# A two-layer convolution kernel: one image's rows on another engine, stores on another queue, two loads swapped, statistics spread over more steps, one sum placed later

## The chip, the cores and the metric

The kernel runs on one core of a Trainium2 chip. The core has five engines with an instruction queue each: TensorE (PE, with its weight loads listed as PEld), VectorE (DVE), ScalarE (ACT), GpSimd (POOL) and SyncE (SP). SP does nothing but issue transfers[...]. All transfers are carried by the same 16 DMA engines. Each engine works through its own queue in order, and waits on semaphores for what others produce.

The metric is the device time of one execution in microseconds (us). The time before is the median of three runs, 2894.33 us (2892.17 to 2900.01).

## The reference

The input `x` has 4 images of 16 channels with 256 by 256 points. Two layers follow each other, each with a group normalization (8 groups of 2 channels) in front and its input added behind:

```python
def _L0_conv_ref(x, conv_w, conv_b):          # conv_w: 400 x 16 x 3 x 3
    out = conv(x, conv_w, padding='SAME') + conv_b[None, :, None, None]
    logits = out.reshape(N, C, K * K, H, W)   # C = 16, K = 5
    weights = jax.nn.softmax(logits, axis=2)
    return jnp.einsum('ncuij,ncuij->ncij', _unfold(x), weights)
...
def _L1_conv_ref(x, base_weight, spline_weight, spline_scaler, bias_weight):
    patches = _extract_patches(x, 3, 1, 1)
    bspl = _b_splines(patches, grid)          # 8 cubic B-splines on a grid of step 0.4
    out = jnp.einsum('bjhwn,ijn->bihw', jax.nn.silu(patches), base_weight.sum(axis=2))
    out = out + jnp.einsum('bjhwns,ijns->bihw', bspl,
                           (spline_weight * spline_scaler[..., None]).sum(axis=2))
    return out + bias_weight[None, :, None, None]
...
x = x + _L0_conv_ref(_gn(x), L0_conv_conv_w, L0_conv_conv_b)
x = x + _L1_conv_ref(_gn(x), L1_conv_base_weight, ...)
```

In layer 0, every point of every channel has 25 logits from a 3x3 convolution; their softmax weights the 5x5 neighbourhood of the normalized point. In what follows, h is the normalized x.

## The kernel before

**Stages.** A set-up loads x and the weights, takes the statistics of images 0 and 1, and normalizes the upper half of image 0. Layer 0 then runs over 64 strips: 4 images, 2 halves of 128 rows, 8 strips of 32 columns. Layer 1 runs over units of 16 rows. A second copy of both layers, for logits too large for a plain exponential, stands behind a branch that these inputs don't take.

**What normalization leaves.** h goes to DRAM scratch in two layouts, by `normalize` (L383). Rows, `hs`: tiles `hsp` are computed by ScalarE at L460 (two channels of a row for all strips with their margins, 128x576), the outer margins are copied from `zpad` (L469, L470), and `put_rows` (L416) stores them. Columns, `hst` and `hsl`: `ht` (L473) is transposed on TensorE into `tp` (L498), copied to `tt` and, rounded, to `hi` (L489), their difference is `lo`, and `put_columns` (L430) stores the three. Edges of the scratch are filled with zeros by the transfers of `zeros` (L399), 13 an image.

**Set-up.** SP issues the loads of x and of the weights, GpSimd those of layer 1's weights (`sw`, `ss`, `bw`, 31 transfers). VectorE takes bn_stats of image 0, then `group_stats` and `factors` give the scale and bias `nrm` (L243 to L246). Then the code calls `zeros(0)` on GpSimd's queue, `prepare0` (layer 0's weights, which GpSimd rearranges at L653 and L654), starts normalizing image 0, takes image 1's bn_stats with steps of that normalization in between, and calls `prepare1` (layer 1's weights: GpSimd's product at L619 and L666, 12 stores `ws<-wb` at L689). How the instructions of the set-up stand on an engine beyond the data they need is left to the framework's scheduler.

**A strip of layer 0.** Eight steps of four columns, 512 steps in all. In a step TensorE computes the logits of the four columns in two halves (L1023 on `am`, the taps of `hst`, L1027 on `an`, the taps of `hsl`, with a row of ones for the bias in `an`, filled at L773), into three PSUM buffers. ScalarE takes the exponential of each half (L1046) into one of four buffers `e`. GpSimd multiplies it with `u`, the rows of h (L1051). VectorE sums e and e times u over the 25 taps (L850) one step behind (`LAG = 1`). At a strip's end a quotient follows: ScalarE sums the denominators with a `Copy` (L864), takes `Ln` (L867) and `Exp` (L869), VectorE does L875, L879 and L886. Every four strips `y` is added to a block `xc` of x and stored to `x1s` in two transfers (L958), and ScalarE takes its statistics for layer 1 with pairs of `z` (L921).

`load_im` loads `am` and `an` for 16 columns (four transfers L787, one L795; for the very first in two halves) and `load_u` loads u for a strip (L808), all in SP's queue, ahead of their use.

**Beside the strips** a generator `ahead` issues one piece of other work a step: the lower half of image 0, then image 1's normalization, and for images 2 and 3 first `measure` (L248), then normalization. `measure` lets ScalarE form sums and squares of x by rows of a partition; at its end TensorE sums them over partitions (product with `ones`), VectorE forms the mean and the deviations `dev` (L290 to L298), TensorE sums these (L300), VectorE forms the variance (L304, L307), GpSimd raises it to the power −1/2 (L309), and `factors` makes `nrm` and `nrz`. A `yield` between them moves what follows by one step, in the queues of all engines.

**Order.** From layer 0 on, `in_order` binds each engine to the order of the program text. `behind(i, name)` puts one instruction behind another. `seeds[0]`, `seeds[1]` and `seeds[2]` name ScalarE's, GpSimd's and VectorE's first instruction of the last strip's end that is put behind the start of layer 1: `seeds[0]`, at L868, is the `Ln` of L867.

Of the kernel before, what the change touches and what calls it, by code (L numbers as in the profile page):

```python
# [34 lines left out]
def conv_preact_kernel(  # L35
# [212 lines left out]
    def measure(b, ptr, tiles, busy):  # L248
        xps = tiles[1]
        n = GC * W  # L250

        def load(q, h):
            if q < C // QC:
                nc.sync.dma_start(
                    xps[h][:, :, PAD : PAD + W],
                    x[b, q * QC : (q + 1) * QC, h * P : (h + 1) * P, :].rearrange(
                        "c p w -> p c w"),
                )

        for h in range(NH):  # L260
            load(0, h)
        for _ in range(3):
            yield
        for q in range(C // QC):
            for h in range(NH):
                for k in range(QC // GC):
                    while busy():
                        yield
                    g = q * (QC // GC) + k
                    v = xps[h][:, k * GC : (k + 1) * GC, PAD : PAD + W]  # L270
                    m, s = (moments[:, t, g, h : h + 1] for t in range(2))
                    nc.scalar.activation(v, v, AF.Identity, accum_out=s)
                    nc.scalar.activation(m, s, AF.Copy, scale=-1.0 / n)
                    nc.scalar.activation(v, v, AF.Square, bias=m, accum_out=s)
                    yield
                load(q + 1, h)

        def small(k, name):
            return stat1.tile([P, k], F32, name=f"{name}_{b}", tag=f"{name}m")

        d = stat1.tile([P, G, NH], F32, name=f"dev_{b}", tag="dev")
        mean, var, rstd = small(G, "mean"), small(G, "var"), small(G, "rstd")
        bank = ptr.tile([P, QG, P], F32, name=f"mps_{b}", tag="tp")
        ps = [bank[:, k, 0 : G * NH] for k in range(2)]
        nc.tensor.matmul(
            ps[0], lhsT=ones, rhs=moments[:, 0].rearrange("p g h -> p (g h)"),
            start=True, stop=True,
        )
        yield
        nc.vector.tensor_reduce(  # L290
            mean, ps[0].rearrange("p (g h) -> p g h", h=NH), AX.X, ALU.add
        )
        nc.vector.tensor_scalar(mean, mean, -1.0 / NH, None, ALU.mult)
        nc.vector.tensor_tensor(
            d, moments[:, 0], mean.unsqueeze(2).to_broadcast([P, G, NH]), ALU.add
        )
        nc.vector.tensor_mul(d, d, d)
        nc.vector.scalar_tensor_tensor(d, moments[:, 1], 1.0 / n, d, ALU.mult, ALU.add)  # L298
        yield
        nc.tensor.matmul(  # L300
            ps[1], lhsT=ones, rhs=d.rearrange("p g h -> p (g h)"), start=True, stop=True
        )
        yield
        nc.vector.tensor_reduce(  # L304
            var, ps[1].rearrange("p (g h) -> p g h", h=NH), AX.X, ALU.add
        )
        nc.vector.tensor_scalar(var, var, 1.0 / NH, EPS, ALU.mult, ALU.add)  # L307
        yield
        nc.gpsimd.tensor_tensor(rstd, var, mhalf, ALU.pow)  # L309
        yield  # L310
        factors(b, mean, rstd)
        yield
# [70 lines left out]
    def normalize(b, ptr, tiles, held=None, copier=None, part=None, dense=False):  # L383
# [64 lines left out]
        def rows(q):  # L448
            for h in read:
                xp = place(q, h) if held is None else held[h][:, q * QC : (q + 1) * QC]  # L450
                if part != 1:
                    hsp = prep.tile([P, NST, QC, SP], F32, name=f"hsp{b}_{q}_{h}", tag="hsp")
                ht = prep.tile([P, QW, W // QW, QC], F32, name=f"ht{b}_{q}_{h}", tag=f"ht{h}")
                hts[q, h] = ht
                for k in range(QC // GC):
                    g = q * (QC // GC) + k
                    kc = slice(k * GC, (k + 1) * GC)
                    how = dict(scale=nrm[b][:, 0, g : g + 1], bias=nrm[b][:, 1, g : g + 1])
                    if part != 1:
                        nc.scalar.activation(  # L460
                            hsp[:, :, kc, :].rearrange("p s c w -> p c s w"),
                            bass.AP(
                                tensor=xp.tensor, offset=xp.offset + k * GC * (W + 2 * PAD),
                                ap=[xp.ap[0], [W + 2 * PAD, GC], [SW, NST], [1, SP]],
                            ),
                            AF.Identity, **how,
                        )
                        if k == QC // GC - 1:
                            nc.scalar.copy(hsp[:, 0, :, 0:PAD], zpad)  # L469
                            nc.scalar.copy(hsp[:, NST - 1, :, PAD + SW :], zpad)  # L470
                            moves.append((4, partial(put_rows, q, h, hsp)))
                        yield
                    nc.scalar.activation(  # L473
                        ht[:, :, :, kc].rearrange("p g w c -> p c w g"),
                        xp[:, kc, PAD : PAD + W].rearrange("p c (w g) -> p c w g", g=QW),
                        AF.Identity, **how,
                    )
                    if k == QC // GC - 1:
                        moves.append((4, partial(load, q + (1 if part is None else 2), h)))
                    yield  # L480
# [85 lines left out]
    with tc.tile_pool(name="prep0", bufs=2) as prep, tc.tile_pool(  # L566
# [43 lines left out]
            )  # L610
        for r in range(2):
            nc.sync.dma_start(wnr[r : r + 1, :], conv_b)
        nm = 3 * C
        sw = pre.tile([P, 3, 9, nm], F32, name="sw")
        ss = pre.tile([P, 3, 9, nm], F32, name="ss")
# [48 lines left out]
        def prepare1():  # L664

            nc.gpsimd.tensor_mul(sw, sw, ss)  # L666
            wc = pre.tile([P, 3, nm], F32, name="wc")
            for d in range(3):
                nc.vector.tensor_reduce(
                    wc[:, d], sw[:, d].rearrange("p k j -> p j k"), AX.X, ALU.add  # L670
                )
            nc.vector.tensor_scalar(wc, wc, -1.0 / 6.0, None, ALU.mult)
            order = pre.tile([P, 2, C, SH], F32, name="order")
            nc.vector.tensor_copy(order, ident.rearrange("p (c h s) -> p h c s", h=2, s=SH))
            wcp = ptr0.tile([P, QG, P], F32, name="wcp", tag="tp").rearrange("p g w -> p (g w)")
            wcp = wcp[:, 0 : 3 * nm]
            nc.tensor.matmul(
                wcp, lhsT=order.rearrange("p h c s -> p (h c s)"),
                rhs=wc.rearrange("p d j -> p (d j)"), start=True, stop=True,
            )  # L680
            wb1 = pre.tile([nm, nm], F32, name="wb1")
            nc.vector.tensor_reduce(wb1, bw.rearrange("p k j -> p j k"), AX.X, ALU.add)
            for r in range(RT):
                nc.vector.tensor_copy(
                    wt[:, r : r + 3, :, r, :], wcp.rearrange("p (d e o) -> p d e o", d=3, e=3)
                )
                for d in range(3):
                    for h in range(2):
                        nc.sync.dma_start(  # L689
                            ws[h * (P // 2) + r + d : (h + 1) * (P // 2) : RD, h, :, r, :],  # L690
                            wb1[d * C : (d + 1) * C].rearrange("p (e o) -> p e o", e=3),
                        )
# [5 lines left out]
        for b in range(2):  # L698
# [16 lines left out]
            mean, rstd = group_stats(stat, pstat, st, f"x{b}")  # L715
            factors(b, mean, rstd)
            if b == 0:
                for f in zeros(0, nc.gpsimd):
                    f()
                prepare0()  # L720
            if b == 1:
                prepare1()
            if b == 0:
                ahead = normalize(0, ptr0, tiles, held, nc.vector.tensor_copy, 0)
# [33 lines left out]
    def layer0(shift):  # L758
# [4 lines left out]
        with tc.tile_pool(name=f"prep{arm}", bufs=2) as prep, tc.tile_pool(  # L763
# [6 lines left out]
            ans = [imp.tile([KT, CI * RP], F32R, name=f"an{n}{arm}", bufs=1) for n in range(NIM)]  # L770
            for t in ans:

                nc.vector.memset(t.bitcast(F32)[0 : 2 * C], 1.0)  # L773
            tiles = norm_tiles(prep)
            strips = [(b, hf, s) for b in range(B) for hf in range(NH) for s in range(NST)]
            nci = SW // CI
# [85 lines left out]
            def seed(n, nd, xc):  # L862
                r = prc.tile([P, C, SW], F32, name=f"r_{n}{arm}", tag="r")
                nc.scalar.activation(  # L864
                    nd[:, 0], nd[:, 0], AF.Copy, accum_out=seen[:, 1, n : n + 1]
                )
                nc.scalar.activation(r, nd[:, 0], AF.Ln, bias=tiny)  # L867
                seeds[:1] = [newest(ACTE)]  # L868
                nc.scalar.activation(  # L869
                    r, r, AF.Exp, scale=-1.0, accum_out=seen[:, 0, n : n + 1]  # L870
                )
                after(1, divide, n, nd, xc, r)
# [78 lines left out]
            def store(n, xc):  # L951
# [16 lines left out]
                    ),  # L968
                )
            )  # L970
            ims = [load_im(0)]
            us = [load_u(0)]
            y = None
            ahead = iter(())
            for n, (b, hf, s) in enumerate(strips):
# [511 lines left out]
```

## Time and profile before

The profiled execution took 2882.99 us; the program's span in it is 2881.0, with 1.99 around it. The median of the three runs is 11.3 us above it.

| what | from | value |
|---|---|---|
| set-up, to the first sum of layer 0 | start of the first L850 | 102.6 us |
| layer 0 | 102.6 to 2002.5 us | 1899.9 us |
| layer 1 | 2002.5 us to the end | 878.5 us |
| busy: PE, DVE, ACT, POOL | page, part 1 | 2691.3, 2763.2, 2204.9, 2665.2 us |
| TensorE's granted clock in the set-up, layer 0, layer 1 | busy times by stage | 0.83, 0.99, 0.98 |
| first am load, first product of TensorE, first exponential | time line | 82.97, 87.68, 91.68 us |
| u of the first strip: issued; first product e times u | time line | 89.52; 99.05 us |

A line of the page's groups reads: line, engine, operation, output <- input, shape, count | busy time, mean of one in ns | idle time of the engine just before, and what ended it. A line of the time line reads: start and length in us, engine, line, operation, names, count, and in brackets the idle time before it with what ended it. A line of the list of waits reads: engine, its instruction <- what it waited for: us in total, times, longest us. "SPq" is SP issuing a transfer, "PEld" a weight load. The table of stages has, for each stretch, its length and the busy time of PE, PEld, DVE, ACT and POOL, then the granted clock, the share of the DMA engines and GB/s.

### The profile page before, as it was taken

What the parts mean: (1) busy time and instruction counts of PE and PEld (TensorE: products, weight loads), DVE (VectorE), ACT (ScalarE), POOL (GpSimd) and SP (SyncE); (2) the same over time, 40 slices, a digit from 0 to 9 for tenths busy, and PEclk for the clock granted to TensorE, in tenths of its full rate; (3) what the DMA queues carried; (4) which work ended last, traced back from release to release, by engine and by line L of the source; (5) the groups of instructions that cost most, each with busy time, mean ns of one, the idle gap of its engine ahead of it and who ended that gap; (6) DMA issues with size and microseconds to landing.
All of it is one profiled execution on the core that took longest, in us unless ns stands there. A gap on an engine that the chain in (4) does not pass through costs nothing.

```text
span 2881.0 us, 39240 instructions
## 1 busy us (share of the span) xinstructions
PE 2691.3 (93%) x14150; PEld 1486.9 (52%) x14150; DVE 2763.2 (96%) x1735; ACT 2204.9 (77%) x3077; POOL 2665.2 (93%) x1096
## 2 busy tenths in 40 slices
PE   2798999998999999899999999995899999999998
PEld 1465666655665666566666666663243343343232
DVE  5699999999999999999999999998999999999996
ACT  5466887686877678688664655647999999999995
POOL 4698999998998999899999999999899999999995
PEclk9899999999999999999999999998999999999999
DMA  8878999985999878699986674865787887787883
GB/s 248 253 244 231 280 288 273 273 245 174 276 289 298 247 231 244 197 307 278 283 252 189 196 225 152 242 195 176 234 250 252 247 251 251 239 261 247 252 250 99
DMA packets 337856, 692.96 MB, mean 241 GB/s; under 512 B 29746, under 2 KB 254468, under 8 KB 287284
## 3 DMA queue, kind: packets, MB, share of 16 engines
q1 hardware_dynamic: 329988, 658.13, 73.8%
q0 software_dynamic: 7664, 32.23, 5.5%
q8 instruction: 114, 1.87, 0.3%
q14 instruction: 90, 0.74, 0.1%
HBM read 533.16 MB, written 121.15 MB: 227 GB/s over the span
## 4 chain that ended last, share of the span: by engine, by line
DVE 47%; PE 23%; issue 10%; ACT 7%; DMA 7%; POOL 5%; SPq 1%; DVEq 0%; ACTq 0%; POOLq 0%
DVE nd L850 36%; PE yp L1353 10%; PE lg L1023 8%; POOL e L1051 3%; DVE ring L182 3%; DVE s L179 3%; PE yp L1362 2%; PE lg L1027 2%; ACT xtc L1188 1%; DVE r1a L1197 1%; ACT xtb L1188 1%; DMA an<-hsl 1%; DVE nd L875 1%; DVE r L879 1%; DVE y L886 1%
## 5 line engine op out<-in xcount | busy, mean ns | idle before, releaser
L1051 POOL TENSOR_TENSOR e<-e,u 128x1600 f32<-128x1600 f32 x512 | 1804.6, 3799 | 77.8 <-ACT e L1046 63.3
L850 DVE TENSOR_REDUCE nd<-e 128x128 f32<-128x3200 f32 x512 | 1757.1, 3476 | 46.8 <-POOL e L1051 46.5
L1023 PE MATMUL lg<-wm,am 128*128 128x400 f32 x4096 | 1738.1, 505 | 65.4 <-ACT e L1046 42.3
L1027 PE MATMUL lg<-wn,an 96*128 96x400 f32 x2048 | 1346.8, 658 | 3.5 <-DMA an<-hsl 3.4
L1046 ACT ACTIVATE e<-lg 128x800 f32<-128x800 f32 x1024 | 823.6, 835 | 548.0 <-DVE nd L850 277.9
L1023 PEld LDWEIGHTS lg<-wm,am 128*128 128x128 f32 x4096 | 760.8, 192 | 388.7 <-ACT e L1046 89.4
L1353 PE MATMUL yp<-ring,wt 128*32 128x512 f32 x6144 | 715.9, 594 | 39.9 <-DVE ring L182 37.5
L1027 PEld LDWEIGHTS lg<-wn,an 96*128 96x128 f32 x2048 | 388.1, 190 | 317.2 <-DMA an<-hsl 12.1
L1353 PEld LDWEIGHTS yp<-ring,wt 128*32 128x32 f32 x6144 | 239.3, 108 | 483.9 <-issue 414.0
L1210 POOL TENSOR_TENSOR s1b<-s1b,r1a 128x1024 f32<-128x1024 f32 (+1 forms) x96 | 192.4, 2039 | 0.0
L1210 POOL TENSOR_TENSOR s1a<-s1a,r1a 128x1024 f32<-128x1024 f32 (+1 forms) x96 | 192.2, 2035 | 0.0
L182 DVE SCALAR_TENSOR_TENSOR ring<-s,s1a 128x1024 f32<-128x1024 f32 x132 | 154.7, 1191 | 0.9
L182 DVE SCALAR_TENSOR_TENSOR ring<-s,s1b 128x1024 f32<-128x1024 f32 (+1 forms) x128 | 151.7, 1206 | 0.3
L921 ACT ACTIVATE z<-xc,nrm 128x256 f32<-128x256 f32 x240 | 143.7, 599 | 4.0
L1210 POOL TENSOR_TENSOR s1a<-s1a,r1b 128x512 f32<-128x512 f32 (+2 forms) x68 | 119.7, 1789 | 2.8 <-ACT s1a L1203 2.8
L1210 POOL TENSOR_TENSOR s1b<-s1b,r1b 128x512 f32<-128x512 f32 x64 | 114.9, 1822 | 0.0
L179 DVE SCALAR_TENSOR_TENSOR s<-xta,cb,s 128x1024 f32<-128x1024 f32 (+2 forms) x90 | 111.1, 1255 | 0.5 <-DMA slb<-x1s 0.4
L1206 POOL TENSOR_TENSOR s1a<-r1b 128x1536 f32<-128x1536 f32 (+1 forms) x31 | 86.6, 2794 | 24.5 <-ACT r1b L1195 24.5
L1206 POOL TENSOR_TENSOR s1b<-r1b 128x1536 f32<-128x1536 f32 (+1 forms) x32 | 86.4, 2700 | 22.5 <-ACT r1b L1195 22.5
L179 DVE SCALAR_TENSOR_TENSOR s<-xtb,cb,s 128x1024 f32<-128x1024 f32 (+2 forms) x85 | 105.9, 1266 | 0.2 <-ACT s L176 0.2
L176 ACT ACTIVATE s<-xta,cb 128x1024 f32<-128x1024 f32 (+2 forms) x90 | 96.5, 1086 | 12.5 <-DVE ring L182 11.0
L179 DVE SCALAR_TENSOR_TENSOR s<-xtc,cb,s 128x1024 f32<-128x1024 f32 (+2 forms) x85 | 105.8, 1266 | 0.0
(209 smaller groups left out, 2275.3 us busy)
## 6 DMA issues: line engine op xcount, KB each, us to landing
am<-hst SPq DMA_DIRECT2D x508, 259.8 KB
u<-hs SPq DMA_DIRECT2D x64, 1440.0 KB
an<-hsl SPq DMA_DIRECT2D x127, 519.5 KB
xta<-x1s SPq DMA_DIRECT2D x40, 1024.0 KB
xtb<-x1s SPq DMA_DIRECT2D x40, 1024.0 KB
xtc<-x1s SPq DMA_DIRECT2D x40, 1024.0 KB
x1s<-xc SPq DMA_DIRECT2D x30, 1024.0 KB
xp<-in_x_dram SPq DMA_DIRECT2D x44, 512.0 KB
```

The costliest lines, as they stand in the source:

```text
L176: nc.scalar.activation(s, t, AF.Square, scale=-0.5, bias=cb)
L179: nc.vector.scalar_tensor_tensor(p, t, cb2, s, ALU.subtract, ALU.mult)
L182: nc.vector.scalar_tensor_tensor(f, p, 0.0, q, ALU.min, op)
L850: nc.vector.tensor_reduce(nd[:, :, :, j : j + JG].rearrange("p t c j -> p t j c"), e.rearrange("p t j m c d -> p t j c m d"), AX.XY, ALU.add,)
L921: nc.scalar.activation(z, v, f, scale=nrm[b][:, 0, g : g + 1], bias=nrm[b][:, 1, g : g + 1], accum_out=st1[b][:, t, g, columns_of(n) : col ...
L1023: nc.tensor.matmul(lg[:, i, :NL], lhsT=am[:, o : o + P], rhs=wm.rearrange("p m c d -> p (m c d)"), start=True, stop=False,)
L1027: nc.tensor.matmul(lg[:, i, :NL], lhsT=an[:, o : o + P], rhs=wn.rearrange("p m c d -> p (m c d)"), start=False, stop=True,)
L1046: nc.scalar.activation(ev, lg[:, :, :NL], AF.Exp)
L1051: nc.gpsimd.tensor_tensor(e[:, 1].rearrange("p j m c d -> p j (m c) d"), e[:, 0].rearrange("p j m c d -> p j (m c) d"), uv, ALU.mult,)
L1206: nc.gpsimd.tensor_tensor(s1(n, a, z), r1(n, a, z), r1(n, a, z), ALU.mult)
L1210: nc.gpsimd.tensor_tensor(s1(n, a, z), s1(n, a, z), r1(n, a, z), ALU.mult)
L1353: nc.tensor.matmul(yp[t * M : (t + 1) * M], lhsT=wt[:, d, e].rearrange("p r o -> p (r o)"), rhs=ring[:, r0 + t * RT + d : r0 + t * RT + d ...
```

## The change

It has five parts, and the line numbers after it are up to 14 higher.

1. Image 0's rows `hsp` of the set-up (`part == 0`) are computed by GpSimd, with `tensor_scalar` in place of ScalarE's `activation`, and their margins are set by GpSimd's `memset`. `zeros(0)` is called earlier, ahead of the loads of `sw`, `ss` and `bw` in GpSimd's queue. `prepare0` is called after the factors of image 1 in place of image 0. The fill of `an` with ones moves from VectorE to GpSimd.
2. The 12 stores of `ws` go from SP's queue to GpSimd's.
3. `load_u(0)` is called before `load_im(0)`.
4. In `measure`, the four groups of the end stand 2, 4, 2 and 4 steps apart; before, 1 step each. What follows, image 2's and image 3's normalization, comes eight steps later.
5. `seeds[0]` is the `Copy` with the sum of the denominators, no longer the `Ln`: the last strip's sum stands behind ScalarE's start of layer 1 too.

```diff
@@ measure
         yield
+        yield
         nc.vector.tensor_reduce(
             mean, ps[0].rearrange("p (g h) -> p g h", h=NH), AX.X, ALU.add
         )
...
         nc.vector.scalar_tensor_tensor(d, moments[:, 1], 1.0 / n, d, ALU.mult, ALU.add)
-        yield
+        for _ in range(4):
+            yield
         nc.tensor.matmul(
             ps[1], lhsT=ones, rhs=d.rearrange("p g h -> p (g h)"), start=True, stop=True
         )
+        yield
         yield
         nc.vector.tensor_reduce(
             var, ps[1].rearrange("p (g h) -> p g h", h=NH), AX.X, ALU.add
         )
         nc.vector.tensor_scalar(var, var, 1.0 / NH, EPS, ALU.mult, ALU.add)
-        yield
+        for _ in range(4):
+            yield
         nc.gpsimd.tensor_tensor(rstd, var, mhalf, ALU.pow)
@@ normalize, rows
                     if part != 1:
-                        nc.scalar.activation(
-                            hsp[:, :, kc, :].rearrange("p s c w -> p c s w"),
-                            bass.AP(
...
-                            ),
-                            AF.Identity, **how,
+                        to = hsp[:, :, kc, :].rearrange("p s c w -> p c s w")
+                        row = bass.AP(
...
                         )
+                        if part == 0:
+                            nc.gpsimd.tensor_scalar(
+                                to, row, how["scale"], how["bias"], ALU.mult, ALU.add
+                            )
+                        else:
+                            nc.scalar.activation(to, row, AF.Identity, **how)
                         if k == QC // GC - 1:
-                            nc.scalar.copy(hsp[:, 0, :, 0:PAD], zpad)
-                            nc.scalar.copy(hsp[:, NST - 1, :, PAD + SW :], zpad)
+                            for v in (hsp[:, 0, :, 0:PAD], hsp[:, NST - 1, :, PAD + SW :]):
+                                if part == 0:
+                                    nc.gpsimd.memset(v, 0.0)
+                                else:
+                                    nc.scalar.copy(v, zpad)
@@ set-up
             nc.sync.dma_start(wnr[r : r + 1, :], conv_b)
+        for z in zeros(0, nc.gpsimd):
+            z()
         nm = 3 * C
...
-                        nc.sync.dma_start(
+                        nc.gpsimd.dma_start(
                             ws[h * (P // 2) + r + d : (h + 1) * (P // 2) : RD, h, :, r, :],
...
             if b == 0:
-                for f in zeros(0, nc.gpsimd):
-                    f()
+                pass
+            if b == 1:
                 prepare0()
-            if b == 1:
                 prepare1()
@@ layer0
-                nc.vector.memset(t.bitcast(F32)[0 : 2 * C], 1.0)
+                nc.gpsimd.memset(t.bitcast(F32)[0 : 2 * C], 1.0)
...
                     nd[:, 0], nd[:, 0], AF.Copy, accum_out=seen[:, 1, n : n + 1]
                 )
+                seeds[:1] = [[
+                    i for i in nc.cur_bb.bb.instructions[-8:] if i.engine == ACTE
+                    and isinstance(i, mybir.InstActivation)
+                ][-1]]
                 nc.scalar.activation(r, nd[:, 0], AF.Ln, bias=tiny)
-                seeds[:1] = [newest(ACTE)]
...
+            us = [load_u(0)]
             ims = [load_im(0)]
-            us = [load_u(0)]
```

## The prediction

> **What bounds the kernel.** I read the busy shares of the page first, then the chain that ended last, then busy times by stage, and then the time lines of the places that the change touches. Of the page:
>
> ```profile
> DVE 47%; PE 23%; issue 10%; ACT 7%; DMA 7%; POOL 5%; SPq 1%; DVEq 0%; ACTq 0%; POOLq 0%
> ...
> L1051 POOL TENSOR_TENSOR e<-e,u 128x1600 f32<-128x1600 f32 x512 | 1804.6, 3799 | 77.8 <-ACT e L1046 63.3
> L850 DVE TENSOR_REDUCE nd<-e 128x128 f32<-128x3200 f32 x512 | 1757.1, 3476 | 46.8 <-POOL e L1051 46.5
> ```
>
> In the table by stages, set-up ends at 102.6 us, with the first reduction, and layer 0 fills what follows up to 2002.5:
>
> ```profile
> 102.60:2002.50 1899.90, 1812.12 (x6344) 1167.42 (x6342) 1875.85 (x753) 1332.94 (x2393) 1832.82 (x569) 0.99 0.81 242
> ```
>
> The third pair is VectorE: 1875.85 of 1899.90 us. GpSimd, the fifth, has 1832.82. VectorE bounds layer 0; GpSimd is 2% behind. A quiet strip takes 28.94 us, eight reductions (3.39 from start to start) and three operations of 0.59. What lengthens VectorE's queue there lengthens the run; what empties another engine's queue costs only as far as VectorE runs dry.
>
> The statistics of image 2, on VectorE:
>
> ```profile
> 678.09 3.48 DVE L850 TENSOR_REDUCE nd<-e 128x128 f32<-128x3200 f32 x1
> 681.48 0.17 DVE L290 TENSOR_REDUCE mean<-mps 128x8 f32<-128x16 f32 x1
> 681.69 0.17 DVE L293 TENSOR_SCALAR mean<-mean 128x8 f32<-128x8 f32 x1
> ...
> 682.31 0.17 DVE L298 SCALAR_TENSOR_TENSOR dev<-moments,dev 128x16 f32<-128x16 f32 x1
> 682.40 3.48 DVE L850 TENSOR_REDUCE nd<-e 128x128 f32<-128x3200 f32 x1
> ...
> 690.58 2.78 DVE L307 TENSOR_SCALAR var<-var 128x8 f32<-128x8 f32 x1
> 693.38 3.49 DVE L850 TENSOR_REDUCE nd<-e 128x128 f32<-128x3200 f32 x1
> ...
> 700.77 1.22 DVE L243 COPY nrm<-rstd 128x8 f32<-128x8 f32 x1
> 701.91 0.24 DVE L244 SCALAR_TENSOR_TENSOR nrm<-mean,rstd 128x8 f32<-128x8 f32 x1
> 702.07 3.56 DVE L246 SCALAR_TENSOR_TENSOR nrz<-rstd 128x8 f32<-128x8 f32 x1
> 705.56 3.48 DVE L850 TENSOR_REDUCE nd<-e 128x128 f32<-128x3200 f32 x1
> ```
>
> and on GpSimd at that time:
>
> ```profile
> 689.82 7.01 POOL L1051 TENSOR_TENSOR e<-e,u 128x1600 f32<-128x1600 f32 x2 [8.98 <-ACT e L1046]
> ...
> 698.43 3.53 POOL L1051 TENSOR_TENSOR e<-e,u 128x1600 f32<-128x1600 f32 x1
> ...
> 702.09 6.99 POOL L1051 TENSOR_TENSOR e<-e,u 128x1600 f32<-128x1600 f32 x2
> ```
>
> The reader is to see two things. VectorE never stands idle: its loss in this strip is 0.92 (681.48 to 682.40), 3.00 (690.38 to 693.38) and 4.79 (700.77 to 705.56), 8.71 in all, which is the strip's length, 37.65, less 28.94. And operations on eight elements take 0.17 us while GpSimd stands idle but 1.22, 2.78 and 3.56 while it works, each ending where a GpSimd product ends (693.33, 701.96, 705.6). The same holds for image 3.
>
> **What the Trainium skill says.** "SBUF — State Buffer", section "SBUF: two separate sides": VectorE and GpSimd share one pair of ports as an exclusive lock; a VectorE operation in a two-port mode, or with two SBUF inputs, waits for the whole GpSimd instruction that holds it. The lines above agree (L246: 3.56; in set-up, with GpSimd idle, 0.15). L1197 doesn't: it too reads two SBUF tensors, one a broadcast column, beside a GpSimd busy nine tenths of the time, and its longest is 1.28 against 1.27 in the median. So not every form is held. "VectorE: DVE Perf Modes", section "The perf-mode tier table", puts float32 copies and tensor_scalar from SBUF in a two-port mode, and a PSUM operand outside it; L243 and L307 were held, L290 and L304 (PSUM) took 0.17.
>
> **The change, part by part.** From the list of waits:
>
> ```profile
> PE mps L300 <- DVE dev L298: 14.7, 2, 7.8
> POOL e L1051 <- DMA u<-hs: 13.9, 1, 13.9
> DVE nd L875 <- ACT r L869: 7.6, 1, 7.6
> ```
>
> *Statistics further apart.* TensorE's product of the deviations is issued one step after the mean, while TensorE runs some three steps ahead of VectorE, so it waited 7.8 and 6.9 us, and GpSimd starved for 8.98 and 7.47. With four steps between them this wait goes. But the starvation cost VectorE only what it waited for a product, about 2.6 us, and it spent that in L307, held until 693.36. In exchange, L293 to L298 ran free because GpSimd was starved; now they meet a busy one. New sum for an image. First group: own time 0.92; L293, of L307's form, half a product (3.5/2 = 1.75); L297 and L298 have two SBUF inputs like L246, and GpSimd takes its next product as soon as one ends, so each can wait a whole one: 3.3 or 6.6. L294 reads a broadcast as L1197 does, so nothing. 6.0 to 9.3. Second group (L304, L307): 0.4 + 1.75 = 2.1. Third (L243, L244, L246): 1.75 + 0.24 + 3.5 = 5.5, L246 as before since GpSimd's L245 still stands just ahead of it. 13.6 to 16.9, less 8.7: +5 to +8. While VectorE is held no e comes free (four buffers), so a third hold finds GpSimd out of work now and then: I take +7, for two images +14. Bounds: +1.5 an image if neither L297 nor L298 is held, and another 2 less if the phases are kind; +8.5 at most. So −1 to +17.
>
> *Normalization of images 2 and 3, eight steps later.* Strips 27 and 43 lost 6.6 and 4.7 us where SP's queue backed up: at 877 to 911 stores of x1s, a put of rows behind ACT's z, zeros (8.17 us in issue) and puts of columns stood ahead of am and an. In the new order the columns meet these bursts twice, in strips 27 and 31, as they did before in 23 (no loss) and 27. I cost it at nothing; bounds −12 (the loss gone) and +10 (another of some 5 us at each image's end, where the last puts now stand just ahead of the next image's loads).
>
> *Rows of image 0 on GpSimd, weight stores on its queue, zeros first, prepare0 later, an's fill.* This takes 16 × 0.855 us (L460) and 16 small copies off ACT, from SP the issues below, and from VectorE two fills of 1.79.
>
> ```profile
> 51.90 8.47 SPq L689 DMA_DIRECT2D ws<-wb  x12
> ```
>
> Against that, VectorE's order now puts image 1's bn_stats ahead of image 0's nrm, so normalization begins only behind image 1's second load (landed at 36.4) and its bn_stats, near 41 us, and not at 33.6; and all rows run in GpSimd's queue behind the weights' preparation. A tensor_scalar of 128x576 isn't in the trace. GpSimd's copies of 258 and 34 elements took 0.39 and 0.24, 0.69 ns an element, so 0.6 for 576; its two-input products take 2.1 ns an element, 1.4. "GPSIMD Engine Reference", section 3.1, has one-input bodies at 1.03 to 1.8 cycles of 1.2 GHz: an estimate of 0.6 to 1.0 with dispatch. I take 0.8. Following the queues with the trace's durations, the last put of columns, which landed at 82.8, lands at 81 (79.8 for 0.6; 83.3 for 1.1; 86.9 for 1.4): −1.8, bounds −3 and +4. GpSimd's queue: zeros' 13 issues now stand before the weights, the 12 stores of some 0.5 behind them; only layer 1 needs these stores.
>
> *u ahead of am.* u was issued at 89.52 after eight am loads and landed 9.4 later; GpSimd waited 13.9 in all. The second exponential of the first product ended at 95.2, so at most 99.05 − 95.3 = 3.8 is to be had; then ACT is what is late. Two am transfers now share the engines with u: I take −3.2, bounds −3.8 and 0. Set-up together: −5, bounds −7 and +4.
>
> *The last strip's sum.* ACT stood 5.5 us on it, and VectorE 7.57 at L875. But layer 1's first VectorE operation reads:
>
> ```profile
> 2012.84 1.29 DVE L179 SCALAR_TENSOR_TENSOR s<-xta,cb,s 128x1024 f32<-128x1024 f32 x1 [0.42 <-DMA slb<-x1s]
> ```
>
> slb's loads are issued once the last reduction ends (2002.53), which doesn't move, and land at 2012.85. So VectorE's 7.6 us become a wait for slb: −0.5, bounds −3 and 0.
>
> Sum: −5 + 14 + 0 − 0.5 = +8.5. Against the profiled execution, 2882.99 (span 2881.0, 1.99 around it), that is 2891.5; the median of the runs, 2894.33, is 11.3 higher, so 2903.
>
> **The rivals.**
> - *A, the forecast*, +8.5, 2903; its own range −1 to +17.
> - *B, the forms of the first group are hardly held*: 2 × 1.5 in place of 14, −5 − 0.5: −2.5, 2892. For it: L1197. Against: L246.
> - *C, the other side: SP's queue.* If rows and columns fall clear of the bursts, the stalls of strips 27 and 43 go (−12), with a lock cost in the middle (+6) and set-up −6: −12, 2882. It decides as soon as the gain there passes the lock's cost less 6. For it: in 23 the same burst cost nothing. Against: the put of rows still stands in the burst of strip 27.
> - *D, the last puts meet the burst of strip 31* ahead of the next image's first loads: +5 an image on top of A: +18, 2912. For it: SP's long issues at 894 to 902. Against: no zeros, rows or x are left in that burst.
> - That the yields don't move the product far enough: excluded by the new order, where it stands four steps behind the deviations.
>
> **How the numbers follow.** Chances: A 0.50, B 0.10, C 0.24, D 0.16. 0.3% is 8.7 us, about what a measurement of this kernel can tell from no change. Three fifths of A's chance lies beyond it, the rest within: slower 0.30 + 0.16 = 0.46; same 0.20 + 0.10 = 0.30; faster 0.24. Range 2880 to 2917: it leaves out the lower part of C and the upper of D.
>
> **What would show it.** Right: no wait of TensorE on dev, GpSimd busy through strip 19, and L293, L297, L298, L307, L243, L246 at 1 to 3.6 us, strips 19 to 21 together 13 to 17 us above three quiet ones. Wrong: L297 and L298 at 0.17 beside a working GpSimd; strips 27 and 43 at 29; a GpSimd row over 1.1 us, or the first product later than 96; L179 at the start of layer 1 ahead of slb.

## The result, and the profile after

The changed kernel took 2902.27 us in the median of 17 runs (2895.95 to 2910.16), the kernel before 2891.99 in 17 runs beside them. The ratio is 1.0036, 95% interval 1.0022 to 1.0050: some 10 us slower, 6 to 14 by the interval. The profiled execution has a span of 2901.5 us against 2881.0. That pair lies 20.5 us apart, more than the medians do, so its parts are read for where time goes, and their sum is not the result. Where a part also varies between executions of kernels that have it alike, the other profiles are named beside it.

From the first sum of layer 0 on, both kernels are compared strip by strip (the time between the starts of the strips' first reductions; a quiet strip takes 28.94 us). The excess of a strip over that, in the two profiles:

| part | before | changed | difference |
|---|---|---|---|
| set-up, to the first sum of layer 0 | 102.6 | 101.3 | −1.3 |
| strips 19 and 20 (statistics of image 2) | 8.7 | 11.2 | +2.5 |
| strips 35 and 36 (statistics of image 3) | 8.0 | 13.8 | +5.8 |
| strips 27 and 43 | 11.3 | 15.2 | +3.9 |
| strips 31, 34 and 47 | 0.0 | 9.0 | +9.0 |
| last sum of layer 0 to layer 1's first L179 (start to start) | 13.8 | 8.5 | −5.3 |
| the rest of layer 1 | 868.2 | 874.7 | +6.5 |

First the places that the prediction showed. VectorE's time line in the changed kernel, the statistics of image 2 (L291 to L310 are L290 to L307 of the kernel before), and below it GpSimd's:

```profile
683.19 0.17 DVE L291 TENSOR_REDUCE mean<-mps 128x8 f32<-128x16 f32 x1
683.39 6.03 DVE L294 TENSOR_SCALAR mean<-mean 128x8 f32<-128x8 f32 x1
689.45 0.18 DVE L295 TENSOR_TENSOR dev<-moments,mean 128x16 f32<-128x16 f32 x1
689.66 0.17 DVE L298 TENSOR_TENSOR dev<-dev 128x16 f32<-128x16 f32 x1
689.87 0.17 DVE L299 SCALAR_TENSOR_TENSOR dev<-moments,dev 128x16 f32<-128x16 f32 x1
689.97 3.48 DVE L861 TENSOR_REDUCE nd<-e 128x128 f32<-128x3200 f32 x1
...
711.72 1.99 DVE L310 TENSOR_SCALAR var<-var 128x8 f32<-128x8 f32 x1
...
732.39 2.27 DVE L243 COPY nrm<-rstd 128x8 f32<-128x8 f32 x1
734.57 0.15 DVE L244 SCALAR_TENSOR_TENSOR nrm<-mean,rstd 128x8 f32<-128x8 f32 x1
734.65 0.15 DVE L246 SCALAR_TENSOR_TENSOR nrz<-rstd 128x8 f32<-128x8 f32 x1
```

```profile
658.01 31.37 POOL L1065 TENSOR_TENSOR e<-e,u 128x1600 f32<-128x1600 f32 x9
695.18 3.52 POOL L1065 TENSOR_TENSOR e<-e,u 128x1600 f32<-128x1600 f32 x1 [5.79 <-ACT e L1060]
699.17 3.52 POOL L1065 TENSOR_TENSOR e<-e,u 128x1600 f32<-128x1600 f32 x1 [0.47 <-ACT e L1060]
```

The operation on eight elements at L294 (L293 before), 0.17 us in the kernel before, takes 6.03. It began inside one GpSimd product and outlasted the end of that one (nine products in 31.37 us put it near 685.9); it ended when the next was through and GpSimd had nothing left (689.38). What follows it runs at 0.17, because GpSimd now waits 5.79 us for an e that a held VectorE could not free. So one operation was held over the end of one product and through the whole next one, and those behind it not at all. In image 3 the same L294 took 8.68, over the ends of two products (near 1173.6 and 1177.1) to the end of a third:

```profile
1171.94 8.68 DVE L294 TENSOR_SCALAR mean<-mean 128x8 f32<-128x8 f32 x1
```

```profile
1163.13 17.46 POOL L1065 TENSOR_TENSOR e<-e,u 128x1600 f32<-128x1600 f32 x5
```

How much the steps apart add is seen over all the profiles. Strips 19 and 20 lost 11.2, 10.5 and 10.5 us and strips 35 and 36 13.8 in each of the three kernels that have the new steps and the old forms (changed, e1, e9 below). In the seven that have the old steps they lost 8.7 to 9.2 and 8.0 to 10.9, but for two cases: 15.7 in e6 and 15.2 in e7, where L246 alone was held for 10.61 us, over three products:

```profile
700.83 10.61 DVE L246 SCALAR_TENSOR_TENSOR nrz<-rstd 128x8 f32<-128x8 f32 x1
```

```profile
700.94 10.47 POOL L1061 TENSOR_TENSOR e<-e,u 128x1600 f32<-128x1600 f32 x3
```

So the new steps add some 2 us in image 2 and 4 in image 3, and one hold of this kind in the kernel before would have outweighed that.

TensorE's wait for `dev` did not go. It is in the list of waits of the changed kernel, halved:

```profile
PE mps L302 <- DVE dev L299: 7.0, 2, 3.5
```

The second place is where the kernel ends its layer 0. VectorE's time line, first one line of the kernel before, then the changed kernel:

```profile
2010.08 0.69 DVE L875 TENSOR_TENSOR nd<-nd,r 128x512 f32<-128x512 f32 x1 [7.57 <-ACT r L869]
```

```profile
2018.33 3.48 DVE L861 TENSOR_REDUCE nd<-e 128x128 f32<-128x3200 f32 x1
2024.05 0.69 DVE L889 TENSOR_TENSOR nd<-nd,r 128x512 f32<-128x512 f32 x1 [2.25 <-ACT r L883]
...
2026.80 1.29 DVE L179 SCALAR_TENSOR_TENSOR s<-xta,cb,s 128x1024 f32<-128x1024 f32 x1 [0.41 <-DMA xtc<-x1s]
```

VectorE's wait falls from 7.57 to 2.25 us, and L179 starts 8.5 us after the start of the last sum; before, it was 13.8. All profiles agree: 13.8 in the five kernels without part 5, 8.5 in the eight with it. The 0.4 us ahead of L179 is there in both kernels, with slb named as its cause in one and xtc in the other. It is no wait for a load: in both traces five instructions that test semaphores stand there on VectorE's queue, one every 0.1 us.

The third is a place that the prediction left out. In layer 1, VectorE tests the sums in `seen` once, first in the kernel before, then in the changed one, with GpSimd's time line of the changed one below:

```profile
2454.31 0.61 DVE L317 TENSOR_SCALAR seen<-seen 128x128 f32<-128x128 f32 x1
```

```profile
2468.96 6.90 DVE L321 TENSOR_SCALAR seen<-seen 128x128 f32<-128x128 f32 x1
```

```profile
2463.43 6.04 POOL L1224 TENSOR_TENSOR s1b<-s1b,r1a 128x1024 f32<-128x1024 f32 x3
2469.40 3.67 POOL L1224 TENSOR_TENSOR s1b<-s1b,r1b 128x512 f32<-128x512 f32 x2
2473.00 2.77 POOL L1220 TENSOR_TENSOR s1a<-r1b 128x1536 f32<-128x1536 f32 x1
```

It took 0.61 us before. Here it stands until GpSimd's run of back-to-back operations is over (2475.8), over the ends of three of them, and the layer falls behind by 6.3 us at that point and stays so to the end. No part of the change touches this operation, and the hold is not the changed kernel's alone: of the five profiles without part 5 it took 0.6 us in three (before, e3, e5) and 6.9 in two (e1, e11), and it was held in all five that have part 5 and this form (6.9 in four, 4.2 in e2). In that sense the profile before was a lucky one; whether part 5, which lets the test begin some 4.5 us earlier after the last sum, makes the hold likelier stays open.

The fourth is SP's queue ahead of strip 31, one of those that had lost nothing before. A put is a store of normalized columns to scratch. In the changed kernel:

```profile
1001.29 5.30 SPq L972 DMA_DIRECT2D x1s<-xc  x1
1006.68 7.73 SPq L798 DMA_DIRECT2D am<-hst  x4
1014.51 0.55 SPq L806 DMA_DIRECT2D an<-hsl  x1
...
1015.74 0.42 SPq L839 DMA_DIRECT2D xc<-in_x_dram  x1
1016.26 8.97 SPq L434 DMA_DIRECT2D hst<-tt  x1
...
1028.59 3.49 SPq L798 DMA_DIRECT2D am<-hst  x4
1032.47 0.55 SPq L806 DMA_DIRECT2D an<-hsl  x1
```

A put of columns takes 8.97 us to issue behind a burst of a store of x1s, loads of am, an and u and the load of xc. The loads of am and an behind the puts are late: VectorE has a gap of 3.4 us, and the chain of waits leads from there through TensorE to the second `an`:

```profile
DVE nd L861 <- POOL e L1065: 3.4, 1, 3.4
```

```profile
1032.47 7.89 DMA an<-hsl
```

In the kernel before, no put stands in that burst:

```profile
1011.16 0.42 SPq L828 DMA_DIRECT2D xc<-in_x_dram  x1
1018.11 4.26 SPq L787 DMA_DIRECT2D am<-hst  x3
```

### The profile page after: what moved, and what is told of

Same layout as the page of the kernel before. It is cut to its first block, busy times and chain, and to the rows that moved or that the text cites. A ratio compares the mean times of both kernels' runs of the same rounds, so it can differ in the third digit from the quotient of the medians.

```text
span 2901.5 us, 39258 instructions
## 1 busy us (share of the span) xinstructions
PE 2702.0 (93%) x14150; PEld 1508.6 (52%) x14150; DVE 2779.2 (96%) x1733; ACT 2193.9 (76%) x3045; POOL 2689.0 (93%) x1142
## 4 chain that ended last, share of the span: by engine, by line
DVE 36%; PE 35%; issue 9%; ACT 8%; DMA 7%; POOL 3%; SPq 1%; DVEq 0%; ACTq 0%; POOLq 0%
DVE nd L861 24%; PE lg L1037 19%; PE yp L1367 8%; PE lg L1041 5%; DVE ring L182 4%; DVE s L179 3%; DMA an<-hsl 2%; POOL e L1065 2%; PE yp L1376 2%; DVE r1a L1211 2%; ACT xta L1202 1%; ACT e L1060 1%; ACT xtc L1202 1%; ACT xtb L1202 1%; DMA xp<-in_x_dram 1%
## 5 line engine op out<-in xcount | busy, mean ns | idle before, releaser
L1367 PEld LDWEIGHTS yp<-ring,wt 128*32 128x32 f32 x6144 | 250.9, 109 | 471.2 <-issue 414.1
L179 DVE SCALAR_TENSOR_TENSOR s<-xta,cb,s 128x1024 f32<-128x1024 f32 (+2 forms) x90 | 111.5, 1261 | 0.5 <-DMA xtc<-x1s 0.4
L179 DVE SCALAR_TENSOR_TENSOR s<-xtb,cb,s 128x1024 f32<-128x1024 f32 (+2 forms) x85 | 106.2, 1272 | 1.2 <-ACT s L176 1.2
L179 DVE SCALAR_TENSOR_TENSOR s<-xtc,cb,s 128x1024 f32<-128x1024 f32 (+2 forms) x85 | 106.2, 1272 | 0.0
```

The lines of the kernel that those rows point to most:

```text
L179: nc.vector.scalar_tensor_tensor(p, t, cb2, s, ALU.subtract, ALU.mult)
L1367: nc.tensor.matmul(yp[t * M : (t + 1) * M], lhsT=wt[:, d, e].rearrange("p r o -> p (r o)"), rhs=ring[:, r0 + t * RT + d : r0 + t * RT + d ...
```

## The experiments

Three theories. *Lock*: VectorE operations whose tensor operands all lie in SBUF wait for GpSimd, here those of the statistics. *Queue*: normalization eight steps later brings puts of columns into bursts of SP. *Supply*: the statistics cost what TensorE and GpSimd lose by waiting; the form of VectorE's operations doesn't matter.

Each ratio is taken against runs of the kernel before beside it; the runs were spread over several chips, so the medians of different rows are not compared.

| run | what it is | median us | ratio to before (95%) |
|---|---|---|---|
| e1_spacing_alone | before + part 4 | 2906.17 | 1.0065 (1.0046, 1.0085) |
| e2_without_spacing | changed, part 4 undone | 2880.75 | 0.9990 (0.9974, 1.0006) |
| e3_shift_alone | before + 8 empty steps | 2902.18 | 1.0060 (1.0038, 1.0082) |
| e4_free_spaced | changed, statistics in PSUM | 2879.30 | 0.9972 (0.9956, 0.9988) |
| e5_sets_only | parts 1 to 3 | 2886.35 | 0.9993 (0.9979, 1.0007) |
| e6_am_first | e2, part 3 undone | 2881.82 | 0.9990 (0.9976, 1.0003) |
| e7_whi_act | e2, one copy on ScalarE | 2881.47 | 0.9985 (0.9969, 1.0002) |
| e8_best | e2, PSUM, whi, seen | 2876.32 | 0.9959 (0.9943, 0.9975) |
| e9_verdict | changed, test on seen to PSUM | 2897.29 | 1.0041 (1.0030, 1.0052) |
| e10_free_three | e8, 3 steps more | 2865.54 | 0.9927 (0.9908, 0.9947) |
| e11_shift_three | before + 3 empty steps | 2891.61 | 1.0021 (1.0011, 1.0032) |

**Which part costs.** e1 puts the new `measure` into the kernel before; e2 puts the old one into the changed kernel.

> The kernel before with part 4 alone (the steps of the statistics apart). Lock theory: strips 19 to 21 and 34 to 36 together 5 to 14 us longer than in the kernel before, with VectorE's tensor_scalar and copies of the statistics at 1 to 7 us beside a working GpSimd. Queue theory: strips 31 and 47 at 32 to 33 us in place of 28.94, 27 and 43 at 34 to 37. Both together: +12 to +22 us on the profile, a ratio of 1.003 to 1.007. If part 4 is not what costs (set-up or layer 1 do): within 4 us of the kernel before.

> The changed kernel with the statistics' steps as before. If part 4 carries the loss: strips 19 to 21 and 35 to 36 as before (95.5 and 65.9 us), 31 and 47 at 28.9, first sum near 101.3, from the last sum of layer 0 to layer 1's first L179 some 5 us less than before; in all 3 to 8 us faster than the kernel before, a ratio of 0.997 to 0.999, less up to 6 us where the tensor_scalar on seen is held again. If parts 1 to 3 carry it: slower than before by 3 us or more.

Part 4 alone is 19 us slower (13 to 25), and without it the changed kernel is level with the kernel before, or a little faster. e1's strips 19 and 20 lost 10.5 us, 35 and 36 13.8, 31 and 47 7.0. Part 4 carries the loss; the other four parts together do not.

**The shift without the spacing.** At the end of the statistics in the kernel before:

```diff
         factors(b, mean, rstd)
-        yield
+        for _ in range(9):
+            yield
```

> The kernel before with eight empty steps at the end of the statistics, so that normalization comes eight steps later while the statistics' own steps stay one apart. Queue theory: strips 31 and 47 at 32 to 33 us, 27 and 43 at 34 to 37, strips 19 and 35 at 37 to 38 as before; +5 to +11 us. Lock theory alone: no difference, within 3 us of the kernel before.

Ratio 1.0060: the shift alone is slower, by 11 to 24 us. In its profile strips 31 and 47 lost 4.5 and 2.9 us and 34 lost 1.9, as queue has it; 19 lost 8.7, as before. The long put stands at the same place of SP's queue, behind the load of xc:

```profile
1010.62 0.42 SPq L829 DMA_DIRECT2D xc<-in_x_dram  x1
1011.14 8.95 SPq L431 DMA_DIRECT2D hst<-tt  x1
```

In all five profiles with the shift of eight steps strips 31 and 47 lost 2.3 to 4.5 us and strip 34 1.8 to 2.0; in the eight others nothing. That profile shows less than the medians do: its span of 2890.1 is 9 us more than before, and the profiled execution is the fastest of its eight. Spacing alone can't be separated from the shift by the ratios: e1 and e3 don't differ within their intervals, and by them the shift alone is enough for the whole loss. That the spacing adds to it is shown by the strips of the profiles only.

**The forms without the lock.** The statistics' small tensors in PSUM, two factors by GpSimd:

```diff
+        meanp, varp = bank[:, 2, 0:G], bank[:, 3, 0:G]
+        dp = bank[:, 2, G : G + G * NH].rearrange("p (g h) -> p g h", h=NH)
...
-        nc.vector.tensor_scalar(mean, mean, -1.0 / NH, None, ALU.mult)
+        nc.vector.tensor_scalar(meanp, meanp, -1.0 / NH, None, ALU.mult)
...
-        nc.vector.tensor_scalar(var, var, 1.0 / NH, EPS, ALU.mult, ALU.add)
+        nc.vector.tensor_scalar(var, varp, 1.0 / NH, EPS, ALU.mult, ALU.add)
...
-        factors(b, mean, rstd)
+        nc.gpsimd.tensor_copy(nrm[b][:, 0], rstd)
+        nc.vector.scalar_tensor_tensor(nrm[b][:, 1], meanp, -1.0, rstd, ALU.mult, ALU.mult)
+        nc.gpsimd.tensor_mul(nrz[b][:, 0], rstd, gsel_sb)
+        nc.gpsimd.tensor_mul(nrz[b][:, 1], rstd, rstd)
+        nc.gpsimd.tensor_scalar(nrz[b][:, 1], nrz[b][:, 1], EPS, None, ALU.mult)
```

> The changed kernel, steps apart as in it, but mean, variance and squared deviations of the statistics in PSUM, so that no VectorE operation of theirs reads SBUF alone, and the copy to nrm and the second factor of nrz by GpSimd. Lock theory: none of these operations over 0.4 us, strips 19 to 21 together 88 to 91 us (98.0 in the changed kernel), 34 to 36 together 88 to 92 (102.6): 15 to 20 us faster than the changed kernel, since 27, 31, 43 and 47 stay as long as there. Supply theory (TensorE's wait for dev and GpSimd's shortage make the loss, the forms don't matter): strips 19 to 21 at 95 or more, within 4 us of the changed kernel.

Its groups, with the columns line, engine, operation, names, shapes, count | busy us, mean ns | idle us before:

```profile
L296 DVE TENSOR_SCALAR mps<-mps 128x8 f32<-128x8 f32 x2 | 0.3, 174 | 0.1
...
L313 DVE TENSOR_SCALAR var<-mps 128x8 f32<-128x8 f32 x2 | 0.3, 167 | 0.1
```

Against the same groups of the changed kernel:

```profile
L294 DVE TENSOR_SCALAR mean<-mean 128x8 f32<-128x8 f32 x2 | 14.7, 7354 | 0.1
L321 DVE TENSOR_SCALAR seen<-seen 128x128 f32<-128x128 f32 x1 | 6.9, 6899 | 0.0
L243 DVE COPY nrm<-rstd 128x8 f32<-128x8 f32 x2 | 4.5, 2249 | 0.0
L310 DVE TENSOR_SCALAR var<-var 128x8 f32<-128x8 f32 x2 | 4.0, 1982 | 0.1
```

The same arithmetic at the same steps takes 0.17 in place of 7.35 and 1.98 us. Strips 19 and 20 lose 1.0 and 0.4 (11.2 in the changed kernel), 35 and 36 the same (13.8); 27, 31, 34, 43 and 47 still lose 20.7. The ratio to the kernel before is 0.9972 against 1.0036, 18 us less. Supply falls, lock holds: what the spacing should have brought comes only when these operations no longer need the ports that GpSimd uses. TensorE's wait for dev, 7.0 us in the changed kernel, is gone from the list of waits as well.

**The last strip's sum.** e5 is e2 with part 5 undone.

```diff
-                seeds[:1] = [[
-                    i for i in nc.cur_bb.bb.instructions[-8:] if i.engine == ACTE
-                    and isinstance(i, mybir.InstActivation)
-                ][-1]]
                 nc.scalar.activation(r, nd[:, 0], AF.Ln, bias=tiny)
+                seeds[:1] = [newest(ACTE)]
```

> Parts 1 to 3 alone (statistics' steps and the place of the last strip's sum as before). If part 5 is worth what the two traces show: from the end of the last sum of layer 0 to layer 1's first L179 10.3 us as in the kernel before, against 5.0 in the run without spacing; 4 to 6 us slower than that run, level with the kernel before or up to 3 us off. If L179 waits for slb whatever ScalarE does, as the prediction had it: no difference between the two.

In the profile VectorE's first r1a of layer 1 (L1197 of the kernel before) starts 15.4 us after the end of the last sum, against 10.1 in e2: 5.3 us, as between the two kernels of the case. Some of it is given back: the test on seen starts 451.2 us after the end of the last sum, against 447.7. In the ratios (0.9993 and 0.9990, from two chips) so few microseconds don't show. (The 10.3 and 5.0 of the expectation are counted to L179 from the end of the sum.)

**The set-up.** e6 puts am's loads ahead of u's again, e7 takes one copy, `whi`, off VectorE.

> The run without spacing, with am's loads ahead of u's again (part 3 undone). As the prediction had it (u ahead is worth 3.2 us): first sum at 104 us, in place of 101.0. If u ahead only takes from am what it gives to u, since both share the transfer engines (first product at 91 in place of 87.7 with the same first issue): first sum at 101 to 103.

> The run without spacing, with the copy of wp to whi on ScalarE in place of VectorE. Lock theory for the set-up: VectorE's first copy to tt starts near 44 in place of 46.6, since it no longer stands behind a copy held by GpSimd's product of sw (3.1 us against 0.37 in the kernel before); the first sum then comes 1 to 3 us earlier than 101.0. If the set-up's end is set by the stores of rows and the two buffers of hsp: first sum at 100.5 to 101.5 all the same.

e6: TensorE's first product of layer 0 starts at 87.52 us in place of 91.08, GpSimd's first at 98.67 in place of 97.44, and the first sum at 102.2 in place of 101.0. Thus u ahead is worth some 1 us, since am arrives 3.6 later (1.2 by this pair; the first sum came at 101.0 to 101.8 in the five profiles with parts 1 to 3 and no other change to the set-up). e7: the copy had stood 3.1 us beside GpSimd's product of sw, and 0.5 suffices on ScalarE, but VectorE's first copy to tt begins at 46.30, as it did (46.48 in e2), and the first sum comes at 101.2. The expectation of lock missed, because the hold did not go: it moved to an operation of image 1's statistics, which took 0.69 us in e2. VectorE in e2, VectorE in e7, and GpSimd in e7:

```profile
41.70 0.69 DVE L160 TENSOR_TENSOR d_x<-d_x,mv_x 128x8 f32<-128x8 f32 x1
```

```profile
42.86 3.52 DVE L160 TENSOR_TENSOR d_x<-d_x,mv_x 128x8 f32<-128x8 f32 x1
```

```profile
42.83 0.64 POOL L662 COPY wp<-wnr 96x80 f32<-96x80 f32 x3
43.44 2.91 POOL L674 TENSOR_TENSOR sw<-sw,ss 128x1296 f32<-128x1296 f32 x1
```

It ended at 46.38, with the same product of sw. So this run doesn't say what the hold costs the set-up.

**A version without the locks.** e8 has the old spacing, the PSUM forms, `whi` on ScalarE, and the test on seen with its output in PSUM:

```diff
-        nc.vector.tensor_scalar(low, low, 1e30, None, ALU.is_lt)
-        nc.vector.tensor_reduce(least, low, AX.X, ALU.min)
+        full = psum()
+        high = full[:, 1 : 1 + low.shape[1]]
+        nc.vector.tensor_scalar(high, low, 1e30, None, ALU.is_lt)
+        nc.vector.tensor_reduce(least, high, AX.X, ALU.min)
...
```

> The run without spacing, with the statistics in PSUM, whi by ScalarE and the test on seen written to PSUM. Lock theory: strips 19 and 35 at 32 to 35 us (37.8 and 39.8 there), as what remains is GpSimd's shortage while TensorE waits for dev; the test on seen at 0.3 (4.2 there); strips 31 and 47 at 28.9; 10 to 16 us faster than the kernel before, a ratio of 0.994 to 0.997. Supply theory: strips 19 and 35 stay at 37 or more.

e10 adds `for _ in range(4)` ahead of the second product only:

> As the run before in this list, with the second product four steps behind the deviations in place of one (normalization three steps later). Lock theory: TensorE's wait for dev is gone and strips 19 and 35 come to 29.5 to 30.5 us. Queue theory: whether 31 and 47 grow depends on whether the last columns meet the burst; three steps later they stand at step 243 and the burst at 244, so I expect up to 3 us each there; ratio 0.992 to 0.997.

e8 lost 6.4 and 7.1 us in strips 19 and 20 and 35 and 36, e10 1.4 in each pair. With the locks gone, TensorE's wait for dev is what the statistics cost, and spacing takes it away; the list of waits has it in e8 and not in e10:

```profile
PE mps L303 <- DVE dev L301: 15.2, 2, 8.1
```

The two pairs of strips in all four combinations:

| | steps one apart | steps further apart |
|---|---|---|
| operands in SBUF | 8.7 and 8.0 (before) | 11.2 and 13.8 (changed) |
| operands in PSUM | 6.4 and 7.1 (e8) | 1.4 and 1.4 (e4, e10) |

In e10, 27 and 43 lost 1.6 and 0.6, 31 and 47 nothing; 22 and 38 lost 3.9 each, and 21, 26 and 37 4.6 together. At 2865.54 us, ratio 0.9927, e10 is 21 us faster than the kernel before and by the ratios some 32 faster than the changed one.

**Three steps alone.** In the kernel before:

> The kernel before with three empty steps at the end of the statistics (eight in the run with the shift alone), nothing else. Queue theory, in the form that what matters is where the columns' puts fall against the bursts of x1s and xc: strips 27 and 43 at 29.5 to 32 in place of 35.5 and 33.6, 31 and 47 at 28.9, and up to 4 us more in strips 22 and 38; 3 to 10 us faster than the kernel before. If any later start costs: slower by 3 us or more, strips 31 and 47 at 31 or more.

A miss: the kernel is 6 us slower (3 to 9). 27 and 43 came down to 0.3 and 2.8 as expected, and 31 and 47 lost nothing, but strips 21, 22, 37 and 38 lost 12.3. In sum layer 0 is only 1.0 us longer in this profile than in the one before. Of the 8.0 us between the two spans, 5.8 stand in layer 1, where the test on seen was held for 6.9, and 1.2 in the set-up, neither of which the empty steps touch. So the miss of the gain is explained (the stalls moved), but the loss in the medians is not. Queue tells where a stall goes, not that one place of the puts is better in sum. In strip 22 the chain of waits leads to ScalarE's rows waiting for a load of x (`ACT hsp L461 <- DMA xp<-in_x_dram`, 6.9 us), with the exponentials behind them: another wait than that of strip 31.

**The test on seen alone**, in the changed kernel:

> The changed kernel, with the test on seen written to PSUM. Lock theory: that operation takes 0.3 in place of 6.9 us, and layer 1, from its first L179 to the end, is 6 to 7 us shorter; 4 to 9 us faster than the changed kernel. If the 6.9 us was hidden beside other work: within 2 us of it.

In the profile the operation takes 0.28 us, and layer 1 from its first L179 on 868.3 us, 6.4 shorter (868.1 and 868.4 in e8 and e10, which have this form too). The ratio is 1.0041 (1.0030 to 1.0052) against 1.0036 (1.0022 to 1.0050): no gain is seen. Whether L321 is held as long in executions without the profiler stays open.

## Why the prediction was right

Direction, size and range held: +8.5 us forecast, 10 measured. The terms held less well than the sum, and that the sum came so close is luck. Of the signs that the prediction named for its mechanism, L293, L307 and L243 were held beside a busy GpSimd; but TensorE still waited on dev, strips 19 to 21 lost 11.2 us and not 13 to 17, L297, L298 and L246 were not held, and strips 31 and 47 stalled as in rival D.

- *Statistics, +14*: right in kind. VectorE, never idle before, lost by losing its quiet moment. In size it is +8.3 in the pair (2.5 and 5.8), some 6 to 7 against the middle of the profiles with the old steps (8.9 and 9.4). The mis-sized term is L293, put at half a product (1.75 us): it took 6.03 and 8.68, held over the end of a product. L297 and L298, put at 3.3 or 6.6 together, took 0.17 each, since the long hold before them had left GpSimd without work. L246 took 0.15 in place of 3.5: L245 no longer stood just ahead of it, and GpSimd had nothing to do from 734.6 on, for 2.5 us. That TensorE's wait for dev would go was wrong (7.0 us remain): a VectorE held for 6 us makes dev late although the product stands four steps behind; with the hold gone and the same spacing (e4) the wait is gone. That it costs little as long as the locks stand was right (e4, e8 and e10 together).
- *Normalization eight steps later, 0*: wrong, and the largest miss: +12.9 in the profile, with the shift alone at 1.0060. What came is what rival D said, at strips 31 and 47 (3.5 and 3.6), plus 1.9 in 34 and 3.9 in 27 and 43. The term's bound of +10 was too small.
- *Set-up, −5*: −1.3 in the pair (the first sum at 102.3 to 103.8 in the four profiles with the old set-up, at 101.0 to 101.8 in the five with the new). Two terms failed. The last put was to land at 81; am's first issue came at 82.73 against 82.97, so nothing was gained there although GpSimd's rows took 0.82 us as estimated; what held the puts there stays open. u ahead was to bring 3.2 and brings some 1 (e6): am arrives 3.6 later for it, where 0.6 was allowed.
- *Last strip, −0.5*: wrong. −5.3 at the transition; the label "DMA slb" beside 0.42 us of idle time was read as a wait that would take over, and what stands there is five tests of semaphores.
- *The test on seen*: missing, +6.3 in the pair of profiles. In part that is the luck of this pair, since the operation is held in e1 and e11 too; e9, which takes the hold away, gained nothing in the medians.

So +8.3 for +14, +12.9 for 0, −1.3 for −5, −5.3 for −0.5, and +6.3 unforeseen: errors of both signs that made the total look better than its parts. In the pair of profiles they come to 20.9, more than twice the forecast; only against the medians does +8.5 stand so well.

## What to carry to other kernels

Before you remove a wait, ask whether the bounding engine is idle in it; if it isn't, ask what runs freely only because another engine is stopped. On an engine that shares ports with a busy neighbour, allow for small operations up to the neighbour's longest run of work and not their own length, and move an operand to PSUM where that is all it takes. An operation that runs free in one profile can be held in the next, so look at several before you call a hold gone or new. Shifting background work by a few steps is a change of its own: try it with empty steps, since transfers fall into other bursts.

## What the runs showed of the hardware

A VectorE operation that reads and writes SBUF can wait past the end of one GpSimd instruction into the following ones, when these come back to back: tensor_scalar on 128x8 took 6.03 and 8.68 us beside products of 3.5, on 128x128 6.90 over the ends of three operations of layer 1, and scalar_tensor_tensor with two SBUF inputs (L246) 10.61 beside three products. Other times one product is all it waits for: L310 took 1.99, to the first end, and L246 3.56 in the other twelve of its fourteen cases in the seven kernels with the old steps and forms. What decides between the two stays open. A tensor_scalar with a PSUM operand took 0.17 (128x8, e4) to 0.28 us (128x128, e9) beside a working GpSimd. The Trainium skill, "SBUF — State Buffer", section "SBUF: two separate sides", has the loser wait for the whole instruction that holds the ports; the runs show that it can be more than one. GpSimd's tensor_scalar with a scale and a bias per partition took 0.82 us for 128x576. A store of 260 KB by SP took 8.97 us to issue behind a burst of stores and loads, where the next ones took some 0.6.
